# Cross-attention on one core: x1 and x2 laid out for rows of 2048 B instead of 8192 B, a first load on another queue, and nine warm-up matmuls for eight

## The chip, the core and the metric

The kernel runs on one core of one Trainium2 chip. The metric is the device time of one execution in microseconds (us). Inputs are rearranged on the host before the execution, outside the time; what the change lays out anew is laid out there.

## What is computed

For each of eight batches, two arrays of 512 channels by 1024 positions come in: `x1` (which is also added to the result) and `x2` (the context).

```python
q = jnp.einsum('bcn,dc->bnd', x1, Wq) + bq
k = jnp.einsum('bcn,dc->bdn', x2, Wk) + bk[:, None]
v = jnp.einsum('bcn,dc->bdn', x2, Wv) + bv[:, None]
attn = jax.nn.softmax(jnp.einsum('bnd,bdm->bnm', q, k), axis=2)
attn_out = jnp.einsum('bcm,bnm->bcn', v, attn)
return attn_out + x1
```

All of it is float32; `q` and `k` have 64 channels, `v` has 512.

## The kernel before, in words

The program is written out by hand, instruction by instruction. Three tables of words, `FIRST` (batch 0), `MIDDLE` (batches 1 to 6) and `LAST` (batch 7), give the order; `follow` calls one method for each word. `oa.7` is method `oa` with argument 7; a word with `+` in front works for the next batch, one with `-` for the batch before, so the batches overlap. The order of the words is the order on every engine and every queue; nothing is sorted later.

The stages of one batch:

- **Loads.** `ldx1(h)` (L148) loads half of `x1` and `ldx2(h)` (L161) half of `x2`, each one transfer of 1024 KB over 128 partitions, issued by SyncE (SP). They go into four buffers of one pool (`"x": 4`). In `MIDDLE` the four loads for the next batch stand among the first words and in the middle: `+ldx1.1`, `+ldx2.0`, `+ldx1.0`, then `+ldx2.1`.
- **Projections.** `Q` and `K` (L201) multiply `x1` and `x2` by the small weights on TensorE. `repeat` (L215) copies the result to the other half of the partitions with a transfer, and `kr`, `kl` (L251) split `k` into a rounded and a low part.
- **Values.** `XH`, `XL`, `VY` (all L369) are three passes that together give `v` in float32 accuracy from faster matmuls on split operands: `xh`, `xl`, `xd` split `x2`, `wh`, `wl`, `wd` split the weights. In batch 0 the first two tiles are multiplied whole instead, `VF` (L362), straight from what was loaded.
- **Scores and softmax.** `S` (L256), maxima over partitions on GpSimd (`T`, L276), `E` (L287) the exponential, `es`, `a1` (L307) and `tot` the sums. `a1` is a transfer from GpSimd's queue that adds half of a quarter's exponentials to the other half.
- **Output.** `R` and `D` (L408) accumulate the output tile `u` (0 to 7) in a PSUM bank of tag `B`, of which there are five, shared with the values' tiles. `lo(u)` (L427) fills an SBUF tile `o` with the bias, `oa(u)` (L430) adds the 256 KB of `x1` for this tile with an accumulating transfer on GpSimd's queue, `ev(u)` (L437, VectorE) reads the PSUM bank, scales it, adds `o`, and so frees the bank; `st(u)` (L447) stores it.

The place between two batches that the prediction speaks of is the start of `MIDDLE`. There `-ev.7` of the batch before stands on VectorE; it waits for the landing of `oa.7`, which was issued at the end of the batch before, while the loads for the batch after are running. The bank that `-ev.7` frees is taken by `XH.4` (L369).

The start, `begin` (called before `FIRST`), issues the first pieces: `hx(c)` (L167) loads a quarter of the first chunk of `x2` (128 KB), `hw(c)` (L172) a quarter of the value weights (256 KB). `hx(0)` and all `hw` are issued by SP, `hx(1..3)` by ScalarE (ACT). Meanwhile TensorE runs eight matmuls on a tile of zeros (L462), in three groups of 3, 3 and 2. The first real matmul is `VF.1.0` and needs `hx(0)` and `hw(0)`.

Transfers share eight semaphores in turn: the ninth transfer that SP or ACT issues waits until the first has landed, and so on.

Of the kernel before, what the change touches and what calls it, by code (L numbers as in the profile page):

```python
# [80 lines left out]
def kernel(  # L81
# [12 lines left out]
    nc = tc.nc  # L94
# [32 lines left out]
    def new(shape, tag, name, dtype=F32):  # L127
        pool = side if tag in SIDE else sb
        return pool.tile(shape, dtype, tag=tag, name=name, bufs=BUFS.get(tag, 1))

    def bank(tag, name):
        return psum.tile([P, H], F32, tag=tag, name=name, bufs=BUFS[tag])

    class Batch:
# [7 lines left out]
            self.B, self.o = {}, {}  # L142

        def ldx1(self, h):
            src = x1[self.b, :, h]
            if not self.first:
                self.x1[h] = t = new([P, CT, H], "x", f"x1_{self.b}_{h}")
                nc.sync.dma_start(t, src)  # L148
                return
            self.x1[h] = []  # L150
            for z in range(2):
                t = new([P, 2, H], f"v{'hl'[z]}{2 + h}", f"x1_0_{h}{z}")
                nc.sync.dma_start(t, src[:, 2 * z : 2 * z + 2])
                self.x1[h].append(t)

        def ldx2(self, h):
            src = x2[self.b, :, ts(h, 2)]
            part = slice(1, 2) if self.first and h == 0 else slice(0, 2)
            if h not in self.x2:
                self.x2[h] = new([P, 2, CT, QN], "x", f"x2_{self.b}_{h}")  # L160
            nc.sync.dma_start(self.x2[h][:, part], src[:, part])  # L161

        def hx(self, c):
            if c == 0:
                self.x2[0] = new([P, 2, CT, QN], "x", "x2_0_0")
            queue = nc.scalar if c else nc.sync
            queue.dma_start(self.x2[0][:, 0, c, :], x2[0, :, 0, c])  # L167

        def hw(self, c):
            if c % 2 == 0:  # L170
# [281 lines left out]
    def begin():  # L452
        for c in range(CT):
            states[0].hx(c)
            states[0].hw(c)
        nc.vector.memset(warm, 0.0)
        nc.vector.memset(spark, 0.0)

        for i, times in enumerate((3, 3, 2)):
            ps = bank("B", f"ps_warm{i}")  # L460
            for k in range(times):
                nc.tensor.matmul(  # L462
                    ps, warm, warm.unsqueeze(1).to_broadcast([P, 4, P]), start=(k == 0), stop=(k == times - 1)
                )
        nc.scalar.activation(spark, spark, AF.Exp)
# [10 lines left out]
    with tc.manual_schedule():  # L476
        begin()
        follow(FIRST, 0)
        for b in range(1, B - 1):
            follow(MIDDLE, b)  # L480
        follow(LAST, B - 1)
# [29 lines left out]
```

## Time and profile before

| | |
|---|---|
| median of three runs | 660.19 us (658.77 to 661.8) |
| the profiled execution's own time | 661.46 us |
| its span, first to last instruction | 659.7 us |
| TensorE (PE) busy | 650.4 us, 2816 matmuls |
| VectorE (DVE), ScalarE (ACT), GpSimd (POOL) busy | 557.0, 433.8, 198.6 us |
| moved by transfers | 90.21 MB in 41480 packets |

The profile is of one execution. Time outside the span is 1.76 us. A weight load of TensorE (PEld) stands apart from the matmul it belongs to and runs beside the matmul before it. A float32 matmul (`VF`, `Q`, `K`) stands as two matmuls and two weight loads in the trace. A list of waits gives, in each line, who waited for whom, then the sum in us, how often, and the longest. A DMA queue's line gives packets, MB, and the time that the packets took as a share of 16 DMA engines over the stretch; a packet is one row of a transfer, or a write of 4 B that signals its end. q0 is GpSimd's queue, q1 SP's, q10 ACT's. A line of a DMA issue ends with the size and the median time from issue to landing.

### The profile page before, as it was taken

The numbers are of one execution on the slowest core, as the hardware profiler recorded it, in microseconds if no ns is written. First come the engines' busy times: TensorE is split into PE (matmuls) and PEld (weight loads), VectorE is DVE, ScalarE is ACT, GpSimd is POOL, SyncE is SP. The second block draws the span as 40 slices with busy tenths as digits, with TensorE's granted clock in tenths as the row PEclk, the third lists the DMA queues.
The fourth block names the chain that finished last, engine by engine and source line by source line (L and its number), as shares of the span: only waits on it lengthen the run. The fifth ranks groups of instructions, "written<-read, shape, count | busy, mean of one in ns | idle before, by whom it ended". The sixth has DMA issues, their size and how long they took to land.

```text
span 659.7 us, 8029 instructions
## 1 busy us (share of the span) xinstructions
PE 650.4 (99%) x2816; PEld 496.3 (75%) x2816; DVE 557.0 (84%) x661; ACT 433.8 (66%) x629; POOL 198.6 (30%) x164
## 2 busy tenths in 40 slices
PE   8999999999999999999999999999999999999997
PEld 3567887677875878858887588875788858888886
DVE  3789998998869978799896997969879799799983
ACT  5688868566666657676576765757657676577731
POOL 0032362232413233132232223412234122433341
PEclk9999999999999999999999999999999999999999
DMA  8455458543595525944459244592445924453465
GB/s 332 117 207 96 94 112 263 158 85 64 117 268 147 93 53 116 314 102 90 96 130 327 40 80 96 143 307 45 81 96 148 305 41 81 97 111 81 80 145 112
DMA packets 41480, 90.21 MB, mean 137 GB/s; under 512 B 13152, under 2 KB 13920, under 8 KB 37728
## 3 DMA queue, kind: packets, MB, share of 16 engines
q0 software_dynamic: 13824, 33.56, 29.6%
q1 hardware_dynamic: 27040, 55.62, 24.5%
q10 hardware_dynamic: 576, 0.52, 0.3%
q8 instruction: 22, 0.36, 0.2%
q14 instruction: 18, 0.15, 0.1%
HBM read 51.91 MB, written 16.78 MB: 104 GB/s over the span
## 4 chain that ended last, share of the span: by engine, by line
PE 54%; DMA 9%; DVE 4%; issue 3%; ACT 2%; SPq 0%; POOL 0%; POOLq 0%; ACTq 0%; DVEq 0%
PE ps_o L408 30%; PE ps_v L369 15%; DMA o<-in_x1T_dram 6%; PE ps_s L256 5%; PE ps_q L201 3%; DMA few<-den 2%; PE ps_k L201 2%; DVE e L284 1%; DVE o L437 1%; DMA out_dram<-o 1%; DVE vl L397 1%; DVE qa L234 1%; ACT k L208 0%; ACT q L208 0%; DVE kl L251 0%
## 5 line engine op out<-in xcount | busy, mean ns | idle before, releaser
L408 PE MATMUL ps_o<-vh,eh 128*128 128x512 f32 x512 | 199.3, 389 | 0.0
L408 PE MATMUL ps_o<-vl,el 128*128 128x512 f32 x512 | 199.2, 389 | 0.0
L408 PE MATMUL ps_o<-vd,ed 128*128 128x512 f32 x512 | 143.0, 391 | 0.1
L321 POOL PARTITION_ALL_REDUCE den<-es x32 | 75.5, 2359 | 172.9 <-DVE es L311 155.5
L408 PEld LDWEIGHTS ps_o<-vd,ed 128*128 128x128 f32 x512 | 95.6, 188 | 23.1 <-ACT e L261 1.7
L408 PEld LDWEIGHTS ps_o<-vh,eh 128*128 128x128 f32 x512 | 96.1, 188 | 20.7 <-ACT eh L291 0.8
L408 PEld LDWEIGHTS ps_o<-vl,el 128*128 128x128 f32 x512 | 96.1, 188 | 19.9
L420 ACT ACTIVATE ps_o<-ps_o 128x512 f32<-128x512 f32 x64 | 37.1, 582 | 89.1 <-PE ps_o L408 88.8
L295 DVE TENSOR_TENSOR el<-e,eh 128x1024 fp32r<-128x1024 f32 x64 | 81.4, 1271 | 11.8 <-ACT eh L291 11.0
L276 POOL PARTITION_ALL_REDUCE top<-max x32 | 41.2, 1289 | 158.5 <-DVE max L272 158.5
L261 ACT COPY e<-ps_s 128x512 f32<-128x512 f32 x128 | 72.5, 593 | 19.2 <-PE ps_s L256 19.1
L300 DVE SCALAR_TENSOR_TENSOR ed<-eh,el 128x1024 fp32r<-128x1024 f32 x64 | 79.2, 1246 | 0.9 <-PE ps_o L408 0.7
L284 DVE TENSOR_TENSOR e<-e,top 128x1024 f32<-128x1024 f32 x64 | 77.2, 1224 | 2.0 <-POOL top L276 1.9
L437 DVE SCALAR_TENSOR_TENSOR o<-ps_o,r,o 128x512 f32<-128x512 f32 (+1 forms) x65 | 47.9, 739 | 35.3 <-DMA o<-in_x1T_dram 25.4
L287 ACT ACTIVATE e<-e 128x1024 f32<-128x1024 f32 x64 | 67.0, 1060 | 14.3 <-DVE e L284 14.2
L430 POOL DMA_DIRECT2D o<-in_x1T_dram x64 | 60.4, 1021 | 46.2 <-ACT o L427 40.9
L369 PE MATMUL ps_v<-wh,xh 128*128 128x512 f32 x248 | 66.2, 393 | 3.2 <-DVE o L437 3.2
L291 ACT ACTIVATE eh<-e 128x1024 fp32r<-128x1024 f32 x64 | 66.1, 1055 | 0.1
L369 PE MATMUL ps_v<-wl,xl 128*128 128x512 f32 x248 | 64.5, 390 | 0.0
L369 PE MATMUL ps_v<-wd,xd 128*128 128x512 f32 x248 | 63.7, 392 | 0.0
L382 ACT ACTIVATE ps_v<-ps_v 128x512 f32<-128x512 f32 x64 | 36.9, 585 | 37.6 <-PE ps_v L369 35.6
L369 PEld LDWEIGHTS ps_v<-wh,xh 128*128 128x128 f32 x248 | 46.1, 188 | 15.2 <-DVE o L437 5.3
(46 smaller groups left out, 855.1 us busy)
## 6 DMA issues: line engine op xcount, KB each, us to landing
x<-in_x_dram SPq DMA_DIRECT2D x29, 1024.0 KB, 11.0
o<-in_x1T_dram POOLq DMA_DIRECT2D x64, 256.0 KB, 4.7
es<-e POOLq DMA_DIRECT2D x32, 512.0 KB, 6.7
out_dram<-o SPq DMA_DIRECT2D x63, 256.0 KB, 4.7
x<-in_x_dram SPq DMA_DIRECT2D x5, 512.0 KB, 7.8
k<-k SPq DMA_DIRECT2D x16, 128.0 KB, 5.0
q<-q SPq DMA_DIRECT2D x16, 128.0 KB, 2.3
w_raw<-in_wvT_dram SPq DMA_DIRECT2D x4, 256.0 KB, 5.1
```

Of the source, the lines that this page charges most:

```text
L261: nc.scalar.copy(self.half[h][:, :, i, :], self.ps[h, i].rearrange("p (q n) -> p q n", q=2))
L276: nc.gpsimd.partition_all_reduce(self.top[Q], self.fold[Q][:, 0, :], P, ReduceOp.max)
L284: nc.vector.tensor_tensor(e, e, top, ALU.subtract)
L287: nc.scalar.activation(self.unit(u), self.unit(u), AF.Exp)
L291: nc.scalar.activation(self.e[u]["h"], self.unit(u), AF.Copy, scale=SPLIT)
L295: nc.vector.tensor_tensor(self.e[u]["l"], self.unit(u), f32(self.e[u]["h"]), ALU.subtract)
L300: nc.vector.scalar_tensor_tensor(e["d"], f32(e["h"]), -1.0 / T, f32(e["l"]), ALU.mult, ALU.add)
L321: nc.gpsimd.partition_all_reduce(self.den[Q], self.es[Q][:, 0, :], P, ReduceOp.add)
L369: nc.tensor.matmul(self.B[j], self.c[j // 2][z][:, c, ts(j % 2, P)], w[z][:, c, :], start=(start and c == 0), stop=(stop and c == CT - 1), ...
L408: nc.tensor.matmul(self.B[u], self.e[u][z][:, m, :], self.v[m // 2, z][:, m % 2, :], start=start, stop=stop, skip_group_check=True,)
L430: nc.gpsimd.dma_start(self.o[u], x1T[self.b, ts(u, P), :], accum_op=ALU.add)
L437: nc.vector.scalar_tensor_tensor(o, self.B[u][:, at], self.share(u), o, ALU.mult, ALU.add)
```

## The change

Three edits.

1. **Layout.** `x1` is laid out in DRAM as batch, half, channel block, partition, 512 positions; before, the four channel blocks of a partition stood next to each other. A load of half of `x1` now reads, for each partition, four rows of 2048 B that lie 256 KB apart; before, it was one row of 8192 B. `x2` is laid out as batch, quarter, pair of channel blocks, partition, 512 values; its loads likewise go in rows of 2048 B. Bytes, destinations and the number of transfers are the same; a load of 1024 KB has 512 rows instead of 128. In batch 0 the halved loads of `x1` and the 512 KB piece of `x2` had rows of 4096 B and now have 2048 B. `hx` keeps rows of 1024 B.
2. **Queue.** `hx(0)` is issued by ACT, ahead of `hx(1..3)`, instead of by SP.
3. **Warm-up.** The third group of warm-up matmuls has three instead of two.

```diff
         def ldx1(self, h):
-            src = x1[self.b, :, h]
+            src = x1[self.b, h].rearrange("c p n -> p c n")
...
         def ldx2(self, h):
-            src = x2[self.b, :, ts(h, 2)]
             part = slice(1, 2) if self.first and h == 0 else slice(0, 2)
             if h not in self.x2:
                 self.x2[h] = new([P, 2, CT, QN], "x", f"x2_{self.b}_{h}")
-            nc.sync.dma_start(self.x2[h][:, part], src[:, part])
+            src = x2[self.b, ts(h, 2)][part].rearrange("k z p c n -> p (k z) (c n)")
+            nc.sync.dma_start(self.x2[h][:, part].rearrange("p k (z c) n -> p (k z) (c n)", z=2), src)
 
         def hx(self, c):
             if c == 0:
                 self.x2[0] = new([P, 2, CT, QN], "x", "x2_0_0")
-            queue = nc.scalar if c else nc.sync
-            queue.dma_start(self.x2[0][:, 0, c, :], x2[0, :, 0, c])
+            nc.scalar.dma_start(self.x2[0][:, 0, c, :], x2[0, 0, c // 2, :, c % 2])
...
-        for i, times in enumerate((3, 3, 2)):
+        for i, times in enumerate((3, 3, 3)):
...
-        "x1": _np.asarray(x).reshape(8, 4, 128, 2, 512).transpose(0, 2, 3, 1, 4),
+        "x1": _np.asarray(x).reshape(8, 4, 128, 2, 512).transpose(0, 3, 1, 2, 4),
...
-        "x2": _np.asarray(ctx_2048).reshape(8, 4, 128, 4, 256).transpose(0, 2, 3, 1, 4),
+        "x2": _np.asarray(ctx_2048).reshape(8, 2, 2, 128, 4, 256).transpose(0, 4, 1, 3, 2, 5),
```

From `hx` on, the changed kernel's line numbers are one lower than those of before. On SP's queue at the start of the program, before (`x2_0_0` is the tile of the first half of `x2` in batch 0, `w_raw0` and `w_raw1` the raw value weights, `wqk_sb` the projections' weights):

```order
L167 DMA x2_0_0_77<-in_x2_dram 128x256
L172 DMA w_raw0_79<-in_wvT_dram 128x512 x2
L172 DMA w_raw1_84<-in_wvT_dram 128x512 x2
L161 DMA x2_0_0_77<-in_x2_dram 128x1024
L175 DMA wqk_sb_67<-in_wqk_dram 128x512
L161 DMA x2_0_1_129<-in_x2_dram 128x2048
```

And after:

```order
L171 DMA w_raw0_79<-in_wvT_dram 128x512 x2
L171 DMA w_raw1_84<-in_wvT_dram 128x512 x2
L161 DMA x2_0_0_77<-in_x2_dram 128x2x512
L174 DMA wqk_sb_67<-in_wqk_dram 128x512
L161 DMA x2_0_1_130<-in_x2_dram 128x4x512
```

The value weights are now SP's first transfers, and the loads of `x2` write two and four pieces of 512 values per partition where they wrote one. On ACT the row of `hx` stands in the same place, ahead of everything else, with four transfers instead of three.

On SP's queue between batches 1 and 2, before (`x1_3_1` is the second half of `x1` of batch 3, `out_0_dram` the output):

```order
L148 DMA x1_3_1_1576<-in_x1_dram 128x2048
L161 DMA x2_3_0_1587<-in_x2_dram 128x2048
L447 DMA out_0_dram<-o_1_5_1450 128x512
L148 DMA x1_3_0_1603<-in_x1_dram 128x2048
L447 DMA out_0_dram<-o_1_6_1493 128x512
L161 DMA x2_3_1_1732<-in_x2_dram 128x2048
```

And after:

```order
L148 DMA x1_3_1_1577<-in_x1_dram 128x4x512
L161 DMA x2_3_0_1588<-in_x2_dram 128x4x512
L446 DMA out_0_dram<-o_1_5_1451 128x512
L148 DMA x1_3_0_1604<-in_x1_dram 128x4x512
L446 DMA out_0_dram<-o_1_6_1494 128x512
L161 DMA x2_3_1_1733<-in_x2_dram 128x4x512
```

The order is the same; only the shape of the loads differs. The order on VectorE and GpSimd is unchanged in the whole program, and on TensorE one warm-up matmul is added before the first `VF`.

## The prediction

> **What bounds the kernel now.** I read the page first, then the list of waits, the chain of waits at the batch boundaries, the DMA view in short windows there, and the timeline of the first 16 us.
>
> ```profile
> PE 650.4 (99%) x2816; PEld 496.3 (75%) x2816; DVE 557.0 (84%) x661; ACT 433.8 (66%) x629; POOL 198.6 (30%) x164
> ```
>
> TensorE is the bound, so time can be won only where it waits or runs slowly. The list of waits has these two for it, its longest for another engine, and above them one of VectorE:
>
> ```profile
> DVE o L437 <- DMA o<-in_x1T_dram: 25.4, 6, 5.6
> ...
> PEld ps_v L369 <- DVE o L437: 5.3, 5, 2.0
> ...
> PE ps_v L369 <- DVE o L437: 3.2, 3, 1.6
> ```
>
> Five times `XH.4` waits for `ev.7` to free its bank, and `ev.7` waits for the landing of `oa.7`. The chain at one boundary shows it: landing, `ev.7`, then TensorE.
>
> ```profile
> 427.37 11.11 DMA o<-in_x1T_dram
> 438.51 0.76 DVE o L437
> 439.31 10.27 PE ps_v L369 x44
> ```
>
> `oa.7` is slow only where it runs beside the loads. These are its size and its time from issue to landing, in the window 185 to 187 us beside them and in 589 to 591 us, where batch 7 has nothing left to load:
>
> ```profile
> o<-in_x1T_dram POOLq DMA_DIRECT2D x1, 256.0 KB, 9.8
> ```
>
> ```profile
> o<-in_x1T_dram POOLq DMA_DIRECT2D x1, 256.0 KB, 4.3
> ```
>
> The second place is the start: first TensorE's matmuls, then its weight loads.
>
> ```profile
> 0.98 3.60 PE L462 MATMUL ps_warm<-warm 128*128 128x512 bf16 x8 [0.98 <-DVE spark L457]
> 5.33 9.18 PE L362 MATMUL ps_v<-w_raw,x 128*128 128x512 f32 x15 [0.75 <-DMA w_raw<-in_wvT_dram]
> ```
>
> ```profile
> 3.10 0.15 PEld L462 LDWEIGHTS <-warm 128*128 128x128 bf16 x1 [0.28 <-issue]
> 3.52 0.15 PEld L462 LDWEIGHTS <-warm 128*128 128x128 bf16 x1 [0.28 <-issue]
> ...
> 8.88 0.34 PEld L362 LDWEIGHTS ps_v<-w_raw,x 128*128 128x128 f32 x1 [0.52 <-issue]
> 9.73 0.34 PEld L362 LDWEIGHTS ps_v<-w_raw,x 128*128 128x128 f32 x1 [0.52 <-issue]
> 10.48 0.19 PEld L362 LDWEIGHTS ps_v<-w_raw,x 128*128 128x128 f32 x1 [0.41 <-issue]
> 10.91 0.19 PEld L362 LDWEIGHTS ps_v<-w_raw,x 128*128 128x128 f32 x1 [0.24 <-issue]
> ...
> 14.34 0.19 PEld L369 LDWEIGHTS ps_v<-wh,xh 128*128 128x128 f32 x1 [0.24 <-issue]
> ```
>
> TensorE stands still for 0.75 us between warm-up and first real matmul. After it, weight loads come every 0.85 us up to 9.73 and every 0.43 from 10.48 on: TensorE runs at half speed until about 10.3 us, 5.0 us after its stream last began.
>
> **The change part by part.** *Layout, at the boundaries.* What matters is how an engine of the 16 shares its time between `oa.7` (queue q0) and the loads (q1). Rows of four windows: 185 to 187 us (loads alone), 180 to 182 (a store in rows of 2048 B, alone), 182 to 184.5 (an `oa`), 191 to 195 (both).
>
> ```profile
> DMA packets 95, 0.72 MB, mean 360 GB/s; under 512 B 7, under 2 KB 7, under 8 KB 7
> ...
> q1 hardware_dynamic: 95, 0.72, 93.7%
> ```
>
> ```profile
> q1 hardware_dynamic: 144, 0.26, 35.0%
> ```
>
> ```profile
> q0 software_dynamic: 143, 0.26, 59.7%
> ```
>
> ```profile
> q1 hardware_dynamic: 190, 0.94, 63.7%
> q0 software_dynamic: 146, 0.29, 40.0%
> ```
>
> A row of 8192 B takes 0.937 x 2 us x 16 / 88 = 0.34 us (7 of the 95 packets are small). A row of 2048 B takes 0.35 x 2 x 16 / 128 = 0.087 us. Four of these are 0.35 us, so I charge the loads nothing for their volume (bound: +3%). A row of `oa` takes 0.597 x 2.5 x 16 / 128 = 0.19 us. An engine has 8 rows of `oa.7` (128 over 16). Alone these are 1.5 us of the 4.3. Beside the loads, landing takes 9.8, 5.5 more. In the last window both queues move near one row for one row. At one for one, 8 rows of a load slip in between: 8 x 0.34 = 2.7 us. The other 2.8 us is then the wait for the first turn, about eight rows of 8192 B that stand ahead.
>
> With rows of 2048 B the slipped-in part becomes 8 x 0.087 = 0.7 us. The first turn costs 0.7 us if eight rows stand ahead as before, and 2.8 if as many bytes do. So `oa.7` lands at 4.3 + 0.7 + (0.7 to 2.8) = 5.7 to 7.8 us after issue, 2.0 to 4.1 sooner. The longest wait of the weight loads is 2.0 us, so all five go. Their price: at most the 5.3 us of the weight loads, at least TensorE's own 3.2; I take the middle, **4.3 us**, since part of a weight load's idle time is covered by the matmul before it. Behind `ev.7` nothing else is late: VectorE sits idle for `oa.7` (25.4 us in six), far longer than TensorE loses.
>
> That one row goes for one whatever its size is shown by the window 3 to 5.5 us, in which ACT's `hx` (1024 B) meets SP's value weights (2048 B):
>
> ```profile
> q1 hardware_dynamic: 295, 0.52, 57.6%
> q10 hardware_dynamic: 298, 0.27, 36.1%
> ```
>
> Equal in rows, two to one in bytes.
>
> Who pays? The loads, if `oa.7` and the `es` transfers behind it on q0 get more turns. The last load, and its first reader:
>
> ```profile
> x<-in_x_dram SPq DMA_DIRECT2D x1, 1024.0 KB, 17.1
> ```
>
> ```profile
> 533.97 1.28 PE ps_k L201 x5
> ```
>
> Issued at about 512.2, it lands at 529.3, and `K` begins at 533.97: 4.7 us of cover. The engines are busy throughout, so the order of rows changes and hardly the end of the last; I charge nothing.
>
> *Queue.* `hw(0)` becomes SP's first transfer and runs beside `hx(0)`. SP's first transfer, issued at 0.73 us, landed 3.2 us later:
>
> ```profile
> 0.73 0.39 SPq L167 DMA_DIRECT2D x<-in_x_dram  x1
> ```
>
> ```profile
> x<-in_x_dram SPq DMA_DIRECT2D x1, 128.0 KB, 3.2
> ```
>
> Rows of `hw` are larger: 8 x (0.087 - 0.048) = 0.3 us (0.048 from q10 above: 0.361 x 2.5 x 16 / 298). So both pieces of the first real matmul are there at about 4.25 us. ACT issues four transfers instead of three, about 0.45 us more. Its next work with a reader, `wh`, waited up to 3.1 us for the weights, which covers it:
>
> ```profile
> ACT wh L184 <- DMA w_raw<-in_wvT_dram: 3.4, 2, 3.1
> ```
>
> *Warm-up.* Nine warm-ups at 0.43 us (the spacing of their weight loads) from 0.98 end at 4.85, after the landing. So the real stream begins at 4.85 instead of 5.33, with no gap. If the switch to full speed comes 5.0 us after the stream began, counted from 0.98 it comes at 6.0. The 16 halves of `VF`: 1.15 us at 0.85 make 1.4 halves, the other 14.6 at 0.43 take 6.3, end 12.3 against 14.34: **2.0 us** sooner. Bounds: nothing, if the switch stays at 10.3 and the weights come no sooner; 2.6 if all 16 run at full speed (4.85 + 6.9 = 11.75). A loss is excluded, since the ninth ends before the real stream begins today. Next in line stand:
>
> ```profile
> 10.02 1.04 ACT L342 ACTIVATE xh<-x 128x1024 fp32r<-128x1024 f32 x1
> 10.97 1.04 ACT L195 ACTIVATE wl<-w_low 128x1024 fp32r<-128x1024 f32 x1
> ```
>
> ```profile
> 11.10 1.23 DVE L347 TENSOR_TENSOR xl<-x,xh 128x1024 fp32r<-128x1024 f32 x1 [0.72 <-ACT xh L342]
> ```
>
> `XH.2` needs `xh` (11.06) at 12.3, `XL.2` needs `wl` (12.01) and `xl` (12.33) about 0.9 us later. Ready in time, with 0.9 to spare; so the 2.0 us passes on.
>
> [...]
>
> *Sum.* 661.46 - 4.3 - 2.0 = 655.2 us against the profiled execution, which is 1.27 above the median. Part of this 1.27 may be the very waits that go, so I take off half: **654.6 us**. The cases below are put on the same footing.
>
> **The rivals.** *A turn belongs to a transfer, not to a row.* Then 32 rows of 2048 B take the turn that 8 rows of 8192 B took, and `oa.7` lands as late as before. For it: the wait for the first turn, 2.8 us, is about one load's share of an engine (8 x 0.34). Against it: a block of eight rows of `oa.7` would be through 1.5 us after its first, while in the window of 191 to 195 its rows run on for the whole 4 us. Only the start's gain is left: 661.46 - 2.0 - 0.6 = 658.9. [...]
>
> *The switch does not move*, because it hangs on something other than an unbroken stream: the start gives 0.3, and 661.46 - 4.3 - 0.3 - 0.6 = 656.3.
>
> *Neither moves:* 660.9, as before.
>
> *Slower: the rows cost more, because each partition now reads from four places 256 KB apart.* The store's 0.087 us is for neighbouring rows; no load with such a pitch is in the trace. The last load has 17.1 us from issue to landing and 4.7 us of cover, so from 1.27 times the row's price on (0.11 us) `K` waits. At 1.5 times the load lands 8.6 us later, `K` waits 3.9 us at six boundaries, 23 us: 661.46 - 2.0 + 23 = 682. [...]
>
> **How the numbers follow.** A measurement of this kernel can tell about 0.5% from no change, so faster means below 656.9 and slower above 663.5. Forecast 0.60 (654.6), turn by transfer 0.16 (658.9), switch unmoved 0.13 (656.3), neither 0.04, slower 0.07. Faster: nearly all of the forecast and two thirds of the unmoved switch, 0.67; same 0.26; slower 0.07. The range: at the low end the upper bounds (661.46 - 5.3 - 2.6 = 653.6) less what the median may lie lower, 652.6; at the high end the turn by transfer is taken in, 659.0. Left out are "neither" and "slower" and the tails of the others, under 2 in 10.
>
> **What would show it.** Right: `oa.7` at the boundaries lands 6 to 8 us after issue, the wait of `ps_v` for `o` L437 is gone from TensorE's list, the gap before `VF` is gone, and weight loads come every 0.43 us from 6 us on. Wrong: `oa.7` still at 9 us or more; `K` waiting for a load of `x`; spacing of 0.85 us until 10; or a new wait of TensorE at the boundaries.

## The result, and the profile after

The changed kernel takes 655.3 us (median of nine runs, 652.67 to 658.21); the kernel before takes 660.19 us beside it (nine runs, 658.75 to 664.66). The ratio is 0.9922, with a 95% interval of 0.9893 to 0.995: 5.1 us less, between 3.3 and 7.1. The forecast was 654.6.

The profiled execution took 654.69 us and has a span of 652.9, 6.8 less than the one of before. TensorE is still the bound:

```profile
PE 646.5 (99%) x2817; PEld 495.7 (76%) x2817; DVE 557.5 (85%) x661; ACT 434.2 (66%) x629; POOL 197.6 (30%) x164
```

The list of waits after, in its order:

```profile
DVE o L436 <- DMA o<-in_x1T_dram: 19.3, 8, 3.7
...
PEld ps_s L255 <- DVE kl L250: 2.3, 3, 1.3
...
PEld ps_v L368 <- DVE o L436: 0.8, 1, 0.8
...
PEld ps_v L368 <- ACT xh L341: 0.7, 1, 0.7
PEld ps_v L361 <- DMA x<-in_x_dram: 0.7, 2, 0.4
...
PEld ps_v L368 <- DVE xl L346: 0.5, 1, 0.5
```

The wait of `ps_v` for `o` fell from 5.3 us in five to 0.8 in one. VectorE still waits for `oa` transfers, 19.3 us where it was 25.4, and TensorE hardly feels it any more. What now stands ahead is a wait of the scores `ps_s` for `kl`, 2.3 us; short ones for `xh`, for `xl` and for a load of `x` (`VF`, L361) are new at the start.

The landing of `oa.7` between batches 5 and 6, after:

```profile
o<-in_x1T_dram POOLq DMA_DIRECT2D x1, 256.0 KB, 8.3
```

Over the six boundaries it lands 7.3 to 9.1 us after its issue, 8.2 in the mean; before, 9.1 to 11.1, 9.8 in the mean. The forecast was 5.7 to 7.8.

The start, TensorE's matmuls and a few weight loads:

```profile
0.98 3.56 PE L461 MATMUL ps_warm<-warm 128*128 128x512 bf16 x9 [0.98 <-DVE spark L456]
4.38 7.03 PE L361 MATMUL ps_v<-w_raw,x 128*128 128x512 f32 x16
11.29 1.19 PE L368 MATMUL ps_v<-wh,xh 128*128 128x512 f32 x4
...
14.60 3.65 PE L200 MATMUL ps_k<-x,wqk_sb 128*64 128x512 f32 x16
```

```profile
3.52 0.15 PEld L461 LDWEIGHTS <-warm 128*128 128x128 bf16 x1 [0.28 <-issue]
3.94 0.11 PEld L461 LDWEIGHTS <-warm 128*128 128x128 bf16 x1 [0.28 <-issue]
4.17 0.41 PEld L361 LDWEIGHTS ps_v<-w_raw,x 128*128 128x128 f32 x2
4.82 0.19 PEld L361 LDWEIGHTS ps_v<-w_raw,x 128*128 128x128 f32 x1 [0.24 <-issue]
```

The stream has no gap, and the spacing of the weight loads halves at 4 us (3.52, 3.94, then 4.17): in this execution the switch to full speed came 3 us after the stream began, not 5. `K` begins at 14.60. In the profile of before it began here:

```profile
17.62 1.08 PE L201 MATMUL ps_k<-x,wqk_sb 128*64 128x512 f32 x4
```

So this pair of profiles shows 3.0 us at the start, where 2.0 were forecast. The experiments show that about half of this is chance.

### The profile page after: what moved, and what is told of

It is laid out like the page before. It is cut to its first block, busy times and chain, and to the rows that moved or that the text cites. A ratio compares the mean times of both kernels' runs of the same rounds, so it can differ in the third digit from the quotient of the medians.

```text
span 652.9 us, 8031 instructions
## 1 busy us (share of the span) xinstructions
PE 646.5 (99%) x2817; PEld 495.7 (76%) x2817; DVE 557.5 (85%) x661; ACT 434.2 (66%) x629; POOL 197.6 (30%) x164
## 3 DMA queue, kind: packets, MB, share of 16 engines
q1 hardware_dynamic: 38672, 55.49, 25.5%
## 4 chain that ended last, share of the span: by engine, by line
PE 75%; DVE 4%; DMA 3%; ACT 2%; SPq 0%; issue 0%; ACTq 0%
PE ps_o L407 41%; PE ps_v L368 21%; PE ps_s L255 7%; PE ps_q L200 3%; PE ps_k L200 2%; DMA few<-den 2%; DMA o<-in_x1T_dram 1%; DVE e L283 1%; DVE vl L396 1%; DVE qa L233 1%; DVE o L436 0%; ACT k L207 0%; ACT q L207 0%; DVE kl L250 0%; DVE el L294 0%; DVE ed L299 0%
## 5 line engine op out<-in xcount | busy, mean ns | idle before, releaser
L436 DVE SCALAR_TENSOR_TENSOR o<-ps_o,r,o 128x512 f32<-128x512 f32 (+1 forms) x65 | 47.8, 739 | 29.7 <-DMA o<-in_x1T_dram 19.3
L368 PEld LDWEIGHTS ps_v<-wd,xd 128*128 128x128 f32 x248 | 46.0, 188 | 14.3 <-issue 4.9
```

Source lines behind the costliest of these rows:

```text
L368: nc.tensor.matmul(self.B[j], self.c[j // 2][z][:, c, ts(j % 2, P)], w[z][:, c, :], start=(start and c == 0), stop=(stop and c == CT - 1), ...
L436: nc.vector.scalar_tensor_tensor(o, self.B[u][:, at], self.share(u), o, ALU.mult, ALU.add)
```

## The experiments

Theory: the gain is the layout's at the boundaries plus the start's, and the two add up. Rivals: all of it is the start's; all of it is the layout's; the row size acts in another way than through `oa.7`.

### The parts by themselves

**Layout alone.** The changed kernel with two edits undone:

```diff
-            nc.scalar.dma_start(self.x2[0][:, 0, c, :], x2[0, 0, c // 2, :, c % 2])
+            queue = nc.scalar if c else nc.sync
+            queue.dma_start(self.x2[0][:, 0, c, :], x2[0, 0, c // 2, :, c % 2])
...
-        for i, times in enumerate((3, 3, 3)):
+        for i, times in enumerate((3, 3, 2)):
```

> The rows of 2048 B alone; the first x2 piece stays on SP's queue and there are eight warm-up matmuls. Theory: the boundaries pay for themselves, whatever the start does. The five waits of weight loads for the o that oa.7 fills go, but the landing of oa.7 stays at 7.5 to 9 us (the wait for the first turn did not shrink), so a short wait is left at one or two boundaries: 3.5 to 4 us less than before. Rival A, all of the gain is the start's: no difference, and oa.7 lands late for another reason than row size. Rival B, layout gives all: 5 us or more.

Measured: 655.09 us against 658.43, ratio 0.9948 (0.9923 to 0.9973): 3.4 us less, 1.8 to 5.1. One boundary wait is left, 1.7 us at the first boundary. As the theory has it, though not all of the 3.4 us need come from the boundaries. In this profile the first piece of `x2` lands at 3.3 us, where the four profiles with rows of 8192 B and the same queues and warm-ups have it at 3.9 to 4.6; the first `VF` begins at 4.5, without a gap, where theirs begins at 5.2 to 5.8. So the layout seems to shorten the start as well. That is one execution, and how much of the 3.4 us it makes is not shown.

**Start alone.** The kernel before with the queue and the ninth matmul, rows of 8192 B.

> The first x2 piece on ScalarE's queue and nine warm-up matmuls, with rows of 8192 B as before. Theory: the first K matmul comes 2 to 3 us sooner than at 17.62 us, and the time is 1.5 to 2.5 us less than before (part of what TensorE wins at the start is lost to waits for xh and xl); the boundaries keep their waits of about 5 us. Rival A: all of the 5 us. Rival B, the start is later absorbed by a wait of the first batch: no difference.

Measured: 658.2 against 658.43 in medians, ratio 0.9979 (0.9959 to 0.9999): 1.4 us less by the ratio, 0.1 to 2.7, while the medians differ by 0.2 only; the theory had 1.5 to 2.5. The boundary waits are there (3.5 us in four) and `oa.7` lands 8.6 to 10.0 us after issue. The sum of both, 4.8 us, is the whole change's 5.1 within the intervals, so they can add up. The rival that gave all to the start falls; the one that gave 5 us or more to the layout lies at the end of the layout's interval and is unlikely rather than excluded.

**The ninth matmul alone** and **the queue alone**, both on the kernel before:

```diff
-        for i, times in enumerate((3, 3, 2)):
+        for i, times in enumerate((3, 3, 3)):
```

> Nine warm-up matmuls alone; the first x2 piece stays on SP's queue. Theory: the value weights still land after the ninth warm-up has ended, a gap of 0.3 to 0.5 us is left in TensorE's stream, and such a gap begins the count for full speed anew: spacing of 0.85 us until about 10 us, no more than 0.3 us won. Rival: what counts is how much TensorE has worked, not that it worked without a gap; then full speed comes at 4 to 6 us and the start wins 2 us.

```diff
-            queue = nc.scalar if c else nc.sync
-            queue.dma_start(self.x2[0][:, 0, c, :], x2[0, :, 0, c])
+            nc.scalar.dma_start(self.x2[0][:, 0, c, :], x2[0, :, 0, c])
```

> The first x2 piece on ScalarE's queue alone; eight warm-up matmuls. Theory: the value weights land at about 3.7 us, before the eighth warm-up ends at 4.5, so the stream has no gap and the switch to full speed comes as with nine: the same 1.5 to 2.5 us less as with both. Rival: the ninth matmul is what fills the gap; then the start wins 0.5 us at most.

Measured: ratios 1.0003 (0.9988 to 1.0017) and 1.0011 (0.9989 to 1.0034), no difference in either. For the ninth the time is as expected, its reason is not: a gap of 0.30 us was left, and full speed came before 6.2 us all the same. For the queue the time is not as expected, although `K` begins earliest of all, at 14.07. This is TensorE at the first boundary with the queue alone, and then the granted clock in two windows:

```profile
112.14 1.30 PE L368 MATMUL ps_v<-wh,xh 128*128 128x512 f32 x4 [1.77 <-DVE o L436]
113.23 1.91 PE L368 MATMUL ps_v<-wl,xl 128*128 128x512 f32 x4
114.94 1.80 PE L368 MATMUL ps_v<-wh,xh 128*128 128x512 f32 x4
116.58 1.08 PE L368 MATMUL ps_v<-wl,xl 128*128 128x512 f32 x4
```

```profile
111.00:114.00 3.00, 1.86 (x6) 1.53 (x7) 2.63 (x4) 0.49 (x1) 0.28 (x1) 0.85 1.07 270
114.00:117.00 3.00, 3.00 (x9) 2.35 (x8) 2.93 (x6) 0.58 (x1) 1.06 (x1) 0.59 1.03 345
```

After the wait for `ev.7` the clock falls to half for about 3.4 us (the columns ahead of the DMA share, 0.85 and 0.59, give (0.15 + 0.41) x 3 / 0.5 = 3.4). Twelve matmuls take 116.58 - 112.14 = 4.44 us from the first wait's end; at full speed they follow each other at 0.23 us, 2.8 in all. The wait of 1.8 us so cost another 1.65. The same stands in the profiles of the ninth matmul alone and of one more kernel below: three of the six executions with rows of 8192 B and `oa.7` in place, none of the seven with smaller rows, whose longest wait there is 1.7 us. For the timed runs without a trace there is the mean granted clock of each, which is 0.997 in the three profiled executions with such a fall. With rows of 8192 B and `oa.7` in place, 48 of 114 runs have 0.996 or 0.997 (nine of the twelve with the queue alone, 13 of 35 of the kernel before beside it); with smaller rows all 51 have 0.999 or more. With the queue alone the nine took 659.7 us in the mean and the three others 657.0; with the ninth matmul alone it is six of twelve, which differ from the other six by 0.3 us only. So the fall probably ate part of the start's gain with the queue alone, and to be spared it is a part of what the layout wins: by an estimate 48 / 114 x 1.65 = 0.7 us a run.

**The kernel before, profiled again,** to see how much of the start is chance.

> The kernel before, profiled once more. Theory: the moment of the switch to full speed falls by chance within some 3 us after the stream has begun anew, so the first K matmul comes anywhere between 15 and 18 us (17.62 in the first profile), while the boundary waits are again about 5 us. Rival: the start is the same in each execution, 17.6 us again.

Measured: 662.85 us, `K` at 17.13. The wait of `ps_v` for `o` is 5.0 us in four. By itself that speaks for neither side; the other kernels with the old start decide it. With the layout alone, `K` begins at 15.07, but there the gap was missing; with `kl` moved on the kernel before (below), at 14.99:

```profile
5.20 0.30 PEld L362 LDWEIGHTS ps_v<-w_raw,x 128*128 128x128 f32 x2 [1.53 <-issue]
5.73 0.19 PEld L362 LDWEIGHTS ps_v<-w_raw,x 128*128 128x128 f32 x1 [0.24 <-issue]
6.16 0.19 PEld L362 LDWEIGHTS ps_v<-w_raw,x 128*128 128x128 f32 x1 [0.24 <-issue]
```

Same start, same gap (0.65 us), and full speed from the first `VF` on. Five executions with the old start have `K` at 17.62, 17.13, 15.56, 15.07 and 14.99, mean 16.1; eight with the new queue have it between 14.07 and 15.04, mean 14.8 over the seven that have the ninth matmul too. The first profile of before was the latest of five. The new start wins 16.1 - 14.8 = 1.3 us in the mean of these few profiles (1.5 without the one of the layout alone), near the 1.4 us of the ratio, by taking away the late cases.

### What the row size does to `oa.7`

**No `oa.7`.** The kernel before, with this ahead in `oa`:

```diff
         def oa(self, u):
+            if u == 7 and not self.final:
+                return
```

> The kernel before without the transfer oa.7 in batches 0 to 6 (the output lacks x1 in these seven tiles); rows of 8192 B, start as before. Theory: the boundary waits are waits for oa.7's landing and nothing stands behind them, so this shows the whole of what any speed-up of oa.7 can bring: 3.2 to 5.3 us less than before, at least as much as the layout alone won (3.4). Rival: VectorE is late there for another reason, or TensorE then waits for kl in the same measure: under 2 us.

Measured: 655.89 against 660.38, ratio 0.9939 (0.9917 to 0.9962): 4.0 us less, 2.5 to 5.5. No wait of `ps_v` for `o` is left in its list. So 4.0 us is about all that a faster `oa.7` can bring. The layout's 3.4 us stand beside it, part of which may be the start's.

**Rows of 1024 B and of 4096 B.** The changed kernel with other layouts (for 1024 B, each channel block's row is cut in two; for 4096 B, two channel blocks stand next to each other), here for `x1` alone:

```diff
...
-        "x1": _np.asarray(x).reshape(8, 4, 128, 2, 512).transpose(0, 3, 1, 2, 4),
+        "x1": _np.asarray(x).reshape(8, 4, 128, 2, 2, 256).transpose(0, 3, 1, 4, 2, 5),
...
```

```diff
...
-        "x1": _np.asarray(x).reshape(8, 4, 128, 2, 512).transpose(0, 3, 1, 2, 4),
+        "x1": _np.asarray(x).reshape(8, 2, 2, 128, 2, 512).transpose(0, 4, 1, 3, 2, 5),
...
```

> The changed kernel with its loads in rows of 1024 B. Theory: the wait for the first turn depends on the bytes that stand ahead and stays near 2.8 us, and what slips in falls from 8 x 0.087 to 8 x 0.048 us: oa.7 lands 7.5 us after issue, 0.3 sooner than with 2048 B; the loads take 10% longer, which K's cover holds: the same as the changed kernel within 1 us, 4.5 to 5.5 us less than before. Rival, the first turn is a number of rows: oa.7 lands at 5.2 us, and the last boundary wait goes too: 1 us less than the changed kernel. Rival, the rows' price decides: K waits for a load, and the time is above the changed kernel's by several us.

> The changed kernel with its loads in rows of 4096 B. Theory: what slips in is 8 x 0.17 = 1.4 us, so oa.7 lands at about 8.5 us, between the changed kernel (8.2) and before (9.9); about a third of the boundary waits is back: 1 to 2 us above the changed kernel, 3 to 4 us less than before. Rival, it is not the row size but that the rows lie apart in DRAM: the same as the changed kernel.

Measured: 655.02 us (ratio to before 0.9928, 0.9905 to 0.9951) and 656.37 (0.9935, 0.9911 to 0.996): neither can be told from the changed kernel's 0.9922. The landing of `oa.7` after its issue, over the six boundaries:

| rows of the loads | mean, us | from, to |
|---|---|---|
| 8192 B (before; start alone) | 9.8; 9.4 | 8.6 to 11.1 |
| 4096 B | 8.4 | 7.7 to 8.9 |
| 2048 B (changed; layout alone) | 8.2; 8.3 | 7.3 to 9.2 |
| 1024 B | 8.3 | 7.9 to 8.7 |

It is a step, not a slope: with the new start, from 8192 to 4096 B 1.0 us, and nothing more below. (With `kl` moved, below, 8192 and 2048 B give 8.8 and 7.9 us.) The rival of the 4096 B run came out, too: its time is the changed kernel's. Rows of 4096, 2048 and 1024 B all lie apart in DRAM and those of 8192 B do not, so that the step comes from the size and not from lying apart is not shown. Two windows of one boundary show more. First the stretch that begins 1.6 us after the issue of `oa.7` (when its first packet goes out where it is alone), in before, after and with 1024 B:

```profile
509.69 0.86 POOL L430 DMA_DIRECT2D o<-in_x1T_dram  x1 [4.37 <-ACT o L427]
```

```profile
DMA packets 125, 0.85 MB, mean 292 GB/s; under 512 B 9, under 2 KB 9, under 8 KB 26
...
q1 hardware_dynamic: 125, 0.85, 98.8%
```

```profile
501.99 0.86 POOL L429 DMA_DIRECT2D o<-in_x1T_dram  x1 [4.32 <-ACT o L426]
```

```profile
DMA packets 428, 0.85 MB, mean 283 GB/s; under 512 B 13, under 2 KB 13, under 8 KB 428
...
q1 hardware_dynamic: 428, 0.85, 88.2%
```

```profile
q1 hardware_dynamic: 765, 0.78, 91.1%
```

There is no line for q0 in any of them (windows of 2.9, 3.0 and 2.9 us): `oa.7` waits about 3 us for its first turn, whatever the rows, while the loads move 0.85, 0.85 and 0.78 MB (0.99 in 2.8 us with 4096 B). In the mean its first packet goes out 4.7, 4.7, 4.9 and 4.7 us after issue with rows of 8192, 4096, 2048 and 1024 B.

Then the stretch in which its rows go out, with 8192, 4096, 2048 and 1024 B:

```profile
q1 hardware_dynamic: 218, 1.02, 64.8%
q0 software_dynamic: 158, 0.32, 40.0%
```

```profile
q1 hardware_dynamic: 179, 0.68, 60.6%
q0 software_dynamic: 131, 0.26, 47.1%
```

```profile
q1 hardware_dynamic: 346, 0.65, 61.0%
q0 software_dynamic: 142, 0.26, 47.2%
```

```profile
q1 hardware_dynamic: 498, 0.59, 60.0%
q0 software_dynamic: 143, 0.26, 49.4%
```

The lines count all packets of a queue: of the 218 of the first, 102 are rows of 8192 B, the rest a store's rows of 2048 B and writes of 4 B. Not row for row: the packets of SP's queue per packet of `oa` rise from 1.4 to 3.5 as the rows shrink. The bytes change far less: 1.02 / 0.32 = 3.2 times as many for the loads with 8192 B, then 2.6, 2.5 and 2.3. So for each byte of `oa` the loads move nearly the same with rows of 4096 B and less, and more with 8192 B, which goes with the step in the table. The windows give sums and not the order on one engine, so how an engine divides its turns between the two queues is not shown.

**Half loads.** What stands ahead of the first turn might be the rest of one transfer. The changed kernel, with each load of batches 1 to 7 in two transfers:

```diff
-                nc.sync.dma_start(t, src)
+                for z in range(2):
+                    nc.sync.dma_start(t[:, 2 * z : 2 * z + 2], src[:, 2 * z : 2 * z + 2])
...
```

> The changed kernel with each 1024 KB load of batches 1 to 7 issued as two transfers of 512 KB, in rows of 2048 B as before. The first packet of oa.7 came 4.4 to 5.2 us after its issue with rows of 1024, 2048, 4096 and 8192 B alike. Theory: what stands ahead is a fixed time of transfers already taken up, whatever they are cut into: still 4.4 to 5.2 us, and landing near 8 us. Rival: what stands ahead is the share of one transfer that an engine has begun (32 x 0.087 = 2.8 us): then it halves, the first packet comes at about 3.2 us, oa.7 lands near 6.7, and the last boundary wait goes: 0.5 to 1 us less than the changed kernel.

Measured: 654.6 us (ratio to before 0.9931, 0.9905 to 0.9957), the same as the changed kernel; the first packet of `oa.7` goes out 4.5 to 5.1 us after issue. In the window after issue only q1 stands again:

```profile
q1 hardware_dynamic: 579, 1.09, 102.9%
```

The rival falls. What the first 3 us consist of stays open: neither row size nor transfer size moves them, and the bytes that go out meanwhile vary from 0.78 to 1.09 MB.

### The wait that stands next

The wait for `kl` appears in the profile of before (1.6 us) as in that of after (2.3). The timeline after, VectorE, ScalarE and the two matmuls, near the end of batch 6:

```profile
546.07 1.06 ACT L246 ACTIVATE kh<-k 128x1024 fp32r<-128x1024 f32 x1 [0.73 <-DMA k<-k]
...
549.09 0.17 DVE L329 RECIPROCAL r<-few 128x2 f32<-128x2 f32 x1 [2.33 <-DMA few<-den]
549.20 1.23 DVE L250 TENSOR_TENSOR kl<-k,kh 128x1024 fp32r<-128x1024 f32 x1
...
550.48 0.50 PE L255 MATMUL ps_s<-qa,kl 128*128 128x512 f32 x1 [0.84 <-DVE kl L250]
```

`kl` could run from 547.1 on, when `kh` is done; it is queued behind `rec.1`, which waits 2.3 us for a transfer of 0.5 KB. **`kl` first** in `MIDDLE`, on the changed kernel (part of the line):

```diff
-D.2.6 rec.1 +kl d.3
+D.2.6 +kl rec.1 d.3
```

> The changed kernel, and in batches 1 to 6 kl stands ahead of rec.1 on VectorE. Theory: the waits for kl (2.3 us of weight loads in the changed kernel) are waits of rec.1 for few.1, a transfer of 0.5 KB that lands 6 to 7 us after issue, behind which kl is queued; with kl ahead they go: 1 to 2 us less than the changed kernel, 6 to 7 us less than before. Rival: kl itself is late (its k comes by a transfer as well), or rec.1 is then late for ev.2: no difference from the changed kernel.

Measured: 652.9 us against 660.38, ratio 0.9891 (0.987 to 0.9912), 7.2 us less than before; the runs lie between 652.48 and 653.14. No wait for `kl` is left:

```profile
547.13 1.23 DVE L250 TENSOR_TENSOR kl<-k,kh 128x1024 fp32r<-128x1024 f32 x1 [0.61 <-ACT kh L246]
548.27 0.16 DVE L329 RECIPROCAL r<-few 128x2 f32<-128x2 f32 x1
```

`rec.1` then finds its data landed. The medians differ from the changed kernel's by 2.4 us, each against its own runs of before by 2.0; the intervals of the two ratios still overlap.

**The same move on the kernel before:**

> The kernel before with kl ahead of rec.1 and nothing else. Theory: the waits for kl are there without the change as well (1.6 us in its profile), and stand apart from those for oa.7: 1.5 to 2.5 us less than before, and much less scatter between the runs. Rival: they appear only once the boundaries are shorter; then the move brings nothing here.

Measured: 656.53 against 658.7, ratio 0.9965 (0.9944 to 0.9985): 2.3 us less. So the wait for `kl` was there without the change and is no wait taken over from the boundaries. The runs still scatter (653.37 to 658.63), against the theory; the profiled one has 2.7 us of wait for `o` at the first boundary and a granted clock of 0.51 in the 3 us behind it, and seven of the twelve runs have a mean clock of 0.996 or 0.997.

**With `w4.0` ahead of `wh.1`** as well, so that `xh` and `xl` come sooner at the start (part of the line):

```diff
-wl.0 wh.1 w4.0 xh.1
+wl.0 w4.0 wh.1 xh.1
```

> The changed kernel with kl ahead of rec.1 and, in batch 0, w4.0 ahead of wh.1 on ScalarE, which stands idle there for 2.5 us until the second half of the weights lands. Theory: xh and xl of batch 0 come 1 us sooner, and TensorE's waits for them (0.7 and 0.5 us in the changed kernel) go: 0.5 to 1 us less than with kl ahead alone (about 652). Rival: a late phase of the clock hides it, since TensorE then comes later than xh and xl: no difference.

Measured: 652.84 us, ratio 0.9905 (0.9882 to 0.9929): no difference from `kl` ahead alone. Its profile has no waits for `xh` and `xl`, but that of `kl` ahead alone has none either: there `xh` begins at 9.47 us, here at 9.33. Here the weight loads come every 0.43 us only from 5.41 on and `XH.2`'s begin at 11.42, after `xh`; `K` begins at 14.71, and at 15.04 with `kl` ahead alone, against 14.60 in the changed kernel. The rival holds.

## Why the prediction was right, and where its steps were not

- **What bounds it** was right: five waits at the boundaries and the start. Without `oa.7` the time falls by 4.0 us, inside the bounds of 3.2 to 5.3.
- **Boundaries, 4.3 us forecast, 3.4 measured** for the layout as a whole. The landing came to 8.2 us, above the range of 5.7 to 7.8. Of the two ends of the first-turn wait the 2.8 us is nearly right (3.1 to 3.3 measured), but the bytes do not set it. The step that failed is that one row goes for one whatever its size. The window from 191 us on, 190 packets to 146, did not show it: 96 of the 190 are rows of 8192 B, the rest a store's rows and writes of 4 B. The window of the start, equal in rows of 1024 and 2048 B, is one of SP's queue with ACT's, and did not carry over to GpSimd's; why those two went row for row stays open. The slipped-in part fell not to 0.7 us: from first packet to landing it is 5.1 us before and 3.4 after, where alone it is 2.8, so 2.3 became 0.6 to 0.9 with all smaller rows alike. In sum 1.6 us sooner instead of 2.0 to 4.1. That took away four waits and left one at the first boundary, since none was longer than 2.0: the right result from waits that were short rather than from a transfer that became fast, and so in part luck. A term was left out: after such a wait the clock can fall to half, at 1.65 us (the queue alone), and with smaller rows it did not (a mean of 0.999 or more in all 51 runs). The profile of before has no such fall, so the prediction could not see it there.
- **The loads' volume, charged at nothing** with a bound of 3%, was right in what it did to the time: no `K` waits for `x`. SP's queue took 24.5% of 16 engines over 659.7 us before and 25.5% over 652.9 after, so 3% more; if all of that is the loads', which were about half of it, they cost some 6% more (an estimate from the pages of the two profiles and the packets' times). The rival with rows 256 KB apart needed 27%.
- **Queue and warm-up, 2.0 us forecast, 1.4 measured** (0.1 to 2.7). The mechanism was right: the gap goes, and the late switch with it. The term was sized on one execution that was the latest of five. "Ready in time, with 0.9 to spare" failed: at 11.29 `XH.2` waited 0.71 for `xh`, and `XL.2` 0.50 for `xl`, since `VF` ended earlier than the 12.3 of the forecast.
- **"Behind `ev.7` nothing else is late"** held at the boundaries; the next wait, for `kl`, stood later in the batch and was there before.
- **The rivals.** Turn by transfer: `oa.7` would land at 9.8 us; it lands at 8.2, and half transfers change nothing. Switch unmoved: refuted by the profiles.
- **Half of the 1.27 us** between the profile and the median was taken off. The profile's own lateness at the start, 17.62 against a mean of 16.1, is 1.5 us, so all of it could have been: the start's gain was counted against a late execution and the correction gave a part of it back. These two errors offset each other in part, and both come from one trace; that 654.6 lies within 1 us of 655.3 owes something to that luck.

## What to carry to other kernels

A short transfer of GpSimd's queue beside long ones of another landed about 1 us sooner here when their rows of 8192 B were cut to 4096 B (9.4 to 8.4 us), and no sooner with smaller ones (8.2 and 8.3); beyond that, issue it earlier or take its reader off the path, since the rest of the delay (3 us here, first packet 4.7 to 4.9 us after issue instead of 1.6) did not depend on how the others were cut. Behind an instruction that waits for a transfer, look for what is queued on the same engine and ready: moving `kl` one place won 2 us, more than the 1.4 us of the queue and the ninth matmul together. And take more than one profile before sizing a term at the start of a program: between two executions of the same start (`K` at 17.62 and 14.99) the clock's switch alone moved it by 2.6 us.

## What the runs showed of the hardware that was not expected

- The switch of TensorE to full speed came at about 4.0 us in the profile of after (the spacing of its weight loads halves between 3.94 and 4.17) and at about 10.4 in that of before (it halves between 9.73 and 10.48), with warm-ups that began at 0.98 us in both. At an old start with a gap of 0.7 us (0.65 to 0.75) it came early, before 5.7 us, with `kl` moved, or late, at about 9.4 and 10.4, in the two profiles of before. A gap of 0.30 us, with the ninth matmul alone, did not hold it up: the weight loads come every 0.43 us from 6.16 on. What sets it early or late at one and the same start is not shown.
- A stop of TensorE for 1.8 us was followed by about 3.4 us at half clock, at a cost of 1.65 us (the queue alone). With the ninth matmul alone and with `kl` moved on the kernel before, the stops ahead of the fall were 2.0 and 2.2 us. Another stop of 1.9 us, in the second profile of before, left the clock at 1.00 (112 to 118 us). So the length of the stop alone does not tell whether the clock falls; what else does is not shown.
- Beside loads that fill the engines, a transfer of GpSimd's queue (`oa.7` at the six boundaries) sends its first packet about 4.7 us after issue instead of 1.6, with rows of 1024 to 8192 B (4.7 to 4.9 in the mean) and transfers of 512 or 1024 KB (4.5 to 5.1 with 512) alike.
